# The last level of ranks as two half levels, in steps over two quads of buckets

## Chip, cores and metric

The kernel runs on one core of a Trainium2 chip. The metric is the device time of one execution in microseconds (us). Before the change it was 2584.67 us, the median of three runs between 2577.09 and 2587.84.

## What is computed

One layer of a graph network on 12,500 nodes of 64 features and 212,500 edges, the edges sorted by `dst`:

```python
def _L0_gnn_ref(h, row, col, dist, eW1, eb1, eW2, eb2, nW1, nb1, nW2, nb2):
    edge_in = jnp.concatenate([h[row], h[col], dist], axis=1)
    e = jax.nn.silu(edge_in @ eW1 + eb1)
    e = jax.nn.silu(e @ eW2 + eb2)
    agg = jax.ops.segment_sum(e, row, num_segments=h.shape[0])
    node_in = jnp.concatenate([h, agg], axis=1)
    return jax.nn.silu(node_in @ nW1 + nb1) @ nW2 + nb2
h = jnp.maximum(_layernorm(x, axis=-1), 0.0)
return x + _L0_gnn_ref(h, src, dst, edge_weight1, ...)
```

The sum goes over `row`, which is `src`, while the edges come sorted by `dst`. So each edge has to be brought to its source node.

## The kernel before, in words

**Blocks.** The edges are taken in 208 blocks of 1024. For a block, `count` (L337) counts on DVE and PE how many edges go to each of NB = 100 buckets of 125 nodes, and gives each edge a rank in its bucket; the running counts lie in SBUF in `base`. `send` (L406) multiplies on PE (`qp`, L418) the `dst` part of the first layer and the edge weight, copies the result on ACT to `qs` (L429, L435) and scatters it row by row to the table `q` in HBM with indirect DMAs on POOL (L442), eight of 128 rows for a full block. `send_all` (L463) cuts this work into pieces, three to a block.

**Levels.** In `q` each bucket has rows for 2304 ranks. `LEVELS` (L54) cuts the ranks into levels: each entry gives the number n of 128-rank tiles, the block after which the level's rows are complete, and a number of spare ranks. Spare ranks that a bucket does not fill are zeros, written in mid-run by `fill` (L106) from the ACT queue; when a level closes, `count` lifts `base` to the level's end (L377). The last level before is `(1, 208, 128)`: 128 ranks, complete after the last block.

**Batches and steps.** A quad is G = 4 buckets; there are 25. A batch is one level of one quad; `fetch` (L484) loads its rows as `qt` and the quad's `src` part of the first layer as `a`, on the SP queue, and in the last level also x and the normalised features for the node update (`nodes_in`, L226). A batch has n steps, each over four tiles of 128 edges: 450 steps in all. The parts of a step are:

- `s_lr` and `s_one_t`: the edges' node numbers, turned to lie along the free axis, compared on DVE with the partition number, which gives `oneT` (125 nodes x 128 edges a tile);
- `s_pt`: on PE `qt` transposed (L532) plus `a` times `oneT` (L538), which adds the source's part of the first layer; then Silu on ACT;
- `s_bias`, `s_p2`: the second layer (L570) and Silu;
- `s_one`: DVE compares node numbers (`one`, L551), and asks for the batch four ahead;
- `s_seg`: on PE the sums over the edges of a tile, `e2` times `one`, into the PSUM tile `seg` (L584; the pool `sg` has two buffers);
- `s_add`: DVE adds `seg` to the sums `aggT` in SBUF (L595); in the last level it also appends the quad's node update `nodes` (L235) to `tails`.

`nodes` is a generator in four parts: z (L242, L245) with Silu on ACT, o (L251), the addition of x on DVE (L254), and the output DMA.

**Order.** The order on PE, DVE, ACT and SP is written by the program itself. In one turn of the loop (L880) the parts of neighbouring steps stand in the order of `turn`; `None` is a hook, four to a turn:

```python
turn = [
    (s_pt, 1), (s_add, -2), (s_one_t, 2), None, (s_bias, 1), (s_p2, 0), (s_one, 0), None, (s_seg, -1), None, (s_lr, 3), None,
]
```

The number says how many steps ahead or behind a part is. At a hook the loop puts in pieces of later blocks, spread so that a goal is met when a level's first load is asked for, and one part of the first of `tails`. The goal for a level that needs the blocks up to `LEVELS[w][1]` is

```python
LEAD = 3 * PIECES
total = PIECES * (nblocks - 2 * FIRST)
goal_of = lambda w: min(PIECES * (LEVELS[w][1] - 2 * FIRST) + LEAD, total)
```

with PIECES = 3, FIRST = 4 and nblocks = 208. A load of rows waits for the last scatter of the block that its level names.

## Time and profile before

| what | value |
|---|---|
| runs | 2577.09, 2584.67, 2587.84 us |
| profiled execution: time | 2577.09 us |
| its span, first to last instruction | 2575.3 us |
| mean granted PE clock | 0.933 |
| busy: PE, PEld (weight loads) | 2162.4, 1981.9 us |
| busy: DVE, ACT, POOL | 2050.7, 1110.8, 1802.1 us |
| chain of waits by engine | PE 33%, DMA 20%, POOL 17%, DVE 14%, issue 9% |
| DMA | 457 MB, 177 GB/s over the span |

PE is the matmuls, PEld the loads of their stationary operands; an f32 matmul shows as two records of each. The span is cut into 40 slices of 64 us; each digit there is the busy share in tenths. In a timeline a row gives the start, the length, engine, line, operation, `out<-in`, the shape and the number of instructions merged, and in brackets how long the engine stood idle before and what released it. Matmuls overlap, so what one costs in a stream is read from the starts and not from the lengths.

### The profile page before, as it was taken

What the parts mean: (1) busy time and instruction counts of PE and PEld (TensorE: products, weight loads), DVE (VectorE), ACT (ScalarE), POOL (GpSimd) and SP (SyncE); (2) the same over time, 40 slices, a digit from 0 to 9 for tenths busy, and PEclk for the clock granted to TensorE, in tenths of its full rate; (3) what the DMA queues carried; (4) which work ended last, traced back from release to release, by engine and by line L of the source; (5) the groups of instructions that cost most, each with busy time, mean ns of one, the idle gap of its engine ahead of it and who ended that gap; (6) DMA issues with size and microseconds to landing.
All of it is one profiled execution on the core that took longest, in us unless ns stands there. A gap on an engine that the chain in (4) does not pass through costs nothing.

```text
span 2575.3 us, 45805 instructions
## 1 busy us (share of the span) xinstructions
PE 2162.4 (84%) x16192; PEld 1981.9 (77%) x16192; DVE 2050.7 (80%) x3413; ACT 1110.8 (43%) x2408; POOL 1802.1 (70%) x1712
## 2 busy tenths in 40 slices
PE   2575676656698898989999889999999999999997
PEld 1453676555588888888888888888899898899986
DVE  5986787766788888888898888888889899886542
ACT  2342343222244444444544444444455554444442
POOL 3777777777777777777777777777777777762110
PEclk9776898778899999999999999999999999999999
DMA  4463565555566665666544444454555556665642
GB/s 103 165 211 130 182 194 186 178 168 174 184 216 215 220 199 172 217 219 216 196 167 165 162 156 164 159 172 165 165 177 177 168 170 195 203 191 175 190 157 73
DMA packets 229455, 456.97 MB, mean 177 GB/s; under 512 B 43543, under 2 KB 87588, under 8 KB 229013
## 3 DMA queue, kind: packets, MB, share of 16 engines
q1 hardware_dynamic: 151033, 282.94, 34.1%
q0 software_dynamic: 53536, 123.03, 13.9%
q10 hardware_dynamic: 24650, 48.00, 6.2%
q8 instruction: 131, 2.15, 0.3%
q14 instruction: 105, 0.86, 0.1%
HBM read 264.26 MB, written 189.54 MB: 176 GB/s over the span
## 4 chain that ended last, share of the span: by engine, by line
PE 33%; DMA 20%; POOL 17%; DVE 14%; issue 9%; ACT 2%; DVEq 0%; SPq 0%; POOLq 0%; ACTq 0%
POOL q L442 17%; DMA q<-qs,to 16%; PE pt L538 7%; PE p L570 7%; PE seg L584 6%; PE qp L418 5%; PE pt L532 3%; DVE oneT L523 2%; DMA qt<-q 2%; PE lr L518 2%; DVE oh L345 2%; DVE each L353 2%; DMA pick<-in_edge_weight_dram 2%; DVE one L551 1%; DVE aggT L595 1%
## 5 line engine op out<-in xcount | busy, mean ns | idle before, releaser
L442 POOL DMA_INDIRECT q<-qs,to x1661 | 1773.0, 1067 | 607.7 <-issue 410.0
L542 ACT ACTIVATE e<-pt 128x512 f32<-128x512 f32 x450 | 268.7, 597 | 933.3 <-PE pt L538 933.3
L538 PE MATMUL pt<-oneT,a 125*128 125x128 f32 (+1 forms) x2400 | 493.4, 341 | 45.5 <-DVE oneT L523 45.4
L570 PE MATMUL p<-w,e 128*128 128x128 f32 x3600 | 502.1, 285 | 0.0
L570 PEld LDWEIGHTS p<-w,e 128*128 128x128 f32 x3600 | 480.8, 200 | 22.2 <-issue 7.4
L584 PE MATMUL seg<-one,e 128*128 128x125 f32 x3600 | 490.8, 281 | 3.0 <-DVE one L551 2.7
L418 PE MATMUL qp<-win,pick 128*128 128x256 f32 x1664 | 432.7, 407 | 61.7 <-DMA pick<-in_edge_weight_dram 40.4
L584 PEld LDWEIGHTS seg<-one,e 128*128 128x128 f32 x3600 | 451.1, 197 | 4.1 <-ACT p L564 1.5
L538 PEld LDWEIGHTS pt<-oneT,a 125*128 125x128 f32 x2400 | 367.3, 200 | 71.9 <-DVE oneT L523 54.3
L418 PEld LDWEIGHTS qp<-win,pick 128*128 128x128 f32 x1664 | 327.0, 206 | 110.5 <-issue 32.3
L429 ACT COPY qs<-qp 128x512 f32<-128x512 f32 x418 | 242.7, 583 | 348.4 <-PE qp L418 280.4
L523 DVE TENSOR_SCALAR oneT<-lr,part 125x512 f32<-125x512 f32 x450 | 335.0, 744 | 32.6 <-PE lr L518 32.3
L353 DVE TENSOR_REDUCE each<-oh 128x100 bf16<-128x800 bf16 x208 | 316.0, 1519 | 7.2
L551 DVE TENSOR_TENSOR one<-nodes,qt 128x500 f32<-128x500 f32 x450 | 302.8, 673 | 0.0
L532 PE MATMUL pt<-ident,qt 128*128 128x128 f32 x1800 | 283.7, 282 | 20.1 <-DVE oneT L523 19.5
L574 ACT ACTIVATE e<-p 128x512 f32<-128x512 f32 x450 | 268.2, 596 | 39.3 <-PE p L570 38.7
L564 ACT COPY p<-b2f 128x512 f32<-128x512 f32 x450 | 266.7, 593 | 0.0
L595 DVE TENSOR_TENSOR aggT<-aggT,seg 128x500 f32<-128x500 f32 x275 | 184.1, 669 | 74.9 <-PE seg L584 74.6
L400 DVE SCALAR_TENSOR_TENSOR to<-rank,offE 128x8 int32<-128x8 f32 x208 | 36.3, 175 | 246.9 <-DMA q<-qs,to 242.7
L518 PE MATMUL lr<-identb,qt 128*125 128x128 bf16 x1800 | 181.6, 225 | 41.9 <-DMA qt<-q 36.3
L532 PEld LDWEIGHTS pt<-ident,qt 128*128 128x128 f32 x1800 | 197.6, 146 | 22.5 <-DVE oneT L523 21.9
L398 DVE TENSOR_REDUCE rank<-mine 128x8 f32<-128x800 f32 x208 | 205.1, 986 | 7.2
(134 smaller groups left out, 1589.8 us busy)
## 6 DMA issues: line engine op xcount, KB each, us to landing
qt<-q SPq DMA_DIRECT2D x150, 576.0 KB
a<-ta SPq DMA_DIRECT2D x300, 256.0 KB
qt<-q SPq DMA_DIRECT2D x150, 288.0 KB
q<-zeros ACTq DMA_DIRECT2D x25, 1080.0 KB
q<-qs,to POOLq DMA_INDIRECT x1661
bc<-dests SPq DMA_DIRECT2D x103, 256.0 KB
q<-zeros ACTq DMA_DIRECT2D x10, 1440.0 KB
win<-tb SPq DMA_DIRECT2D x208, 58.0 KB
```

The costliest lines, as they stand in the source:

```text
L353: nc.vector.tensor_reduce(each, oh.rearrange("p t b -> p b t"), AX.X, OP.add)
L418: nc.tensor.matmul(qps[t // 2][:, t % 2, :k], pick[:, t * P : (t + 1) * P], win[:, :k], start=True, stop=True)
L442: ins = nc.gpsimd.indirect_dma_start(out=q[:], out_offset=bass.IndirectOffsetOnAxis(ap=to[:k, j : j + 1], axis=0), in_=qs[:k, t % 2, a, :] ...
L523: nc.vector.tensor_scalar(oneT, st[k].pop("lr")[:L], part1[:L, :], None, op0=OP.is_equal)
L532: nc.tensor.matmul(pt[:, t, :], qt[:, j, :H], ident, is_transpose=True, start=t == 0, stop=False, skip_group_check=True)
L538: nc.tensor.matmul(pt[:, cols, :], a[:L, b, :], oneT[:, cols, :], start=False, stop=True, skip_group_check=True)
L542: nc.scalar.activation(e1, pt, AF.Silu)
L551: nc.vector.tensor_tensor(one.rearrange("p (b j) l -> p b j l", j=n), nodes1[:, None, None, :].to_broadcast(wide), loc[:, tiles[0][1] : ti ...
L564: nc.scalar.copy(p2, b2f)
L570: nc.tensor.matmul(p2[:, t, :], e1[:, t, :], w2, start=False, stop=t == G - 1, skip_group_check=True)
L574: nc.scalar.activation(e2, p2, AF.Silu)
L584: nc.tensor.matmul(item[2][:, b, :], e2[:, t, :], one[:, t, :], start=j < G, stop=j >= G * (n - 1))
```

## The change

The last entry of `LEVELS` becomes two of half a tile, 64 ranks each, complete after blocks 205 and 208, both with 64 spare ranks. For these two levels a batch takes two quads (the 25th quad stands alone), so that there are 13 batches of one step in each and 451 steps in all. A tile of 128 edges now holds 64 ranks of one bucket in its first half and 64 of another in its second half. So:

- `fetch` loads each quad's rows in two DMAs of 64 partitions, and `a` for eight buckets in one DMA, in its own pool of three buffers; `fetch_to` asks for batches NH = 3 ahead where they have two quads, and loads what the node update needs one batch ahead, in the second half level only;
- in `s_pt` each tile has two matmuls of 64 columns with `a` of two buckets;
- in `s_seg` each tile has two matmuls of 64 rows, one for each half, into two PSUM tiles; `s_add` adds both;
- a hook takes up to two parts from the first of `tails`.

The running counts in SBUF, the two buffers of `sg` and the loads of the edge weights ahead of the counts, which the change's short description names as well, are the same in both kernels.

```diff
-LEVELS += [(1, 184, 0), (1, 194, 32), (1, 202, 96), (1, 208, 128)]
-ENDS = [P * sum(n for n, _, _ in LEVELS[: w + 1]) for w in range(len(LEVELS))]
+LEVELS += [(1, 184, 0), (1, 194, 32), (1, 202, 96), (0.5, 205, 64), (0.5, 208, 64)]
+ENDS = [int(P * sum(n for n, _, _ in LEVELS[: w + 1])) for w in range(len(LEVELS))]
...
-        batches = [(w, B, n) for w, (n, _, _) in enumerate(LEVELS) for B in range(NB // G)]
-        steps = [(w, B, n, g) for w, B, n in batches for g in range(n)]
+        batches = []
+        for w, (n, _, _) in enumerate(LEVELS):
+            m = 2 if n < 1 else 1
+            batches += [(w, B, n, min(m, NB // G - B)) for B in range(0, NB // G, m)]
+        number = {(w, B): i for i, (w, B, _, _) in enumerate(batches)}
+        steps = [(w, B, n, g) for w, B, n, _ in batches for g in range(max(1, n))]
...
+            rows = G * int(n * P)
+            for b in range(B, B + m):
+                at = b * G * ROWS + G * ENDS[c] - rows
+                if n < 1:
+                    for h in range(2):
+                        part_ = q[at : at + rows, :].rearrange("(r h j) w -> r h (j w)", h=2, j=2)[:, h, :]
+                        to = qt[h * HB : (h + 1) * HB, 2 * (b - B) : 2 * (b - B) + 2, :]
+                        load_ready(c, nc.sync.dma_start(to.rearrange("p j w -> p (j w)"), part_).ins)
...
+            a = (ld2 if m == 1 else ld3[0]).tile([P, m * G, H], F32, name=f"a{m}")
+            nc.sync.dma_start(a, ta_buckets[:, B * G : (B + m) * G])
...
+        def fetch_to(i):
+
+            while fetched[0] < len(batches) and fetched[0] <= i + (NQ if batches[fetched[0]][3] == 1 else NH):
+                fetch(fetched[0])
+                fetched[0] += 1
+            while fetched[1] < min(fetched[0], i + NH - 1):
+                _, B, _, m = batches[fetched[1]]
+                for b in range(B, B + m):
+                    node_in[b] = nodes_in(b, ndp[0])
+                fetched[1] += 1
...
+            for t, h in itertools.product(range(nt), range(2)) if steps[k][2] < 1 else ():
+                cols = slice(h * HB, (h + 1) * HB)
+                b = t // 2 * G + 2 * h + t % 2
+                nc.tensor.matmul(
+                    pt[:, t, cols], a[:L, b, :], oneT[:, t, cols], start=False, stop=True, skip_group_check=True
+                )
...
+                item[2] = [sgp.tile([P, G, L], F32, name="seg") for _ in range(2 if n < 1 else 1)]
             e2, one = st[k].pop("e2"), st[k].pop("one")
+            for t, h in itertools.product(range(len(tiles)), range(2)) if n < 1 else ():
+                rows = slice(h * HB, (h + 1) * HB)
+                nc.tensor.matmul(
+                    item[2][h][:, t, :], e2[rows, t, :], one[rows, t, :], start=True, stop=True
+                )
...
+            for h, seg in enumerate(segs):
+                v = aggT[:, B * G : (B + m) * G, :]
+                if n < 1:
+                    v = v.rearrange("p (q h j) l -> p h q j l", h=2, j=2)[:, h]
+                    seg = seg[:, : 2 * m, :].rearrange("p (q j) l -> p q j l", j=2)
...
-                    if tails and next(tails[0], 0) == 0:
-                        tails.pop(0)
+                    for _ in range(min(2, len(tails))):
+                        if tails and next(tails[0], 0) == 0:
+                            tails.pop(0)
```

## Prediction

> **What bounds the kernel now.** I read first the page's row of slices, to see which engine is full when.

> ```profile
> PE   2575676656698898989999889999999999999997
> POOL 3777777777777777777777777777777777762110
> PEclk9776898778899999999999999999999999999999
> ```

> POOL shows a steady 7 until about slice 36 (some 2300 us) and then nothing: a 7 that never moves is an engine that never pauses for long. POOL's own timeline says so, at the place where this ends:

> ```profile
> 2250.84 0.96 POOL L442 DMA_INDIRECT q<-qs,to  x1 [0.30 <-DMA q<-qs,to]
> ...
> 2328.59 0.97 POOL L442 DMA_INDIRECT q<-qs,to  x1 [14.78 <-ACT qs L435]
> ```

> Up to 2297 us POOL issues scatter after scatter with 0.30 us between. From record to record, in hundreds from the first at 49 us on, the mean interval is 1.34 to 1.40 us, with one slower hundred at the start. So until 2297 us POOL sets the pace. After that it waits 4 to 15 us at a time for ACT, which waits for PE; its last scatter starts at 2397 us. Who is full then is in the windows (length, then PE, PEld, DVE, ACT, POOL busy, granted clock, DMA share, GB/s):

> ```profile
> 2200.00:2297.00 97.00, 88.57 (x767) 85.38 (x766) 85.37 (x140) 45.44 (x94) 73.37 (x71) 0.98 0.62 197
> 2297.00:2400.00 103.00, 102.05 (x951) 100.93 (x950) 70.39 (x117) 50.54 (x104) 30.34 (x30) 1.00 0.56 177
> 2414.00:2545.00 131.00, 131.00 (x1074) 116.06 (x1072) 52.84 (x90) 54.65 (x112) 15.97 (x22) 1.00 0.49 154
> ```

> From 2297 us on PE is busy all the time at full clock, and nothing else is near full: the last two levels are paced by PE alone, its instructions in order. So each instruction added to PE there lengthens the run, and nothing is gained by readier data. The price of a turn of the step loop is read from PE's timeline, as the start of one row less the start of the next. First a turn of the last level but one, then one of the last level, which carries a quad's node update (z, z, o) too:

> ```profile
> 2405.31 0.39 PE L518 MATMUL lr<-identb,qt 128*125 128x128 bf16 x4
> 2405.54 0.61 PE L532 MATMUL pt<-ident,qt 128*128 128x128 f32 x4
> 2405.98 1.06 PE L538 MATMUL pt<-oneT,a 125*128 125x128 f32 x8
> 2406.88 1.06 PE L570 MATMUL p<-w,e 128*128 128x128 f32 x8
> 2407.77 1.06 PE L584 MATMUL seg<-one,e 128*128 128x125 f32 x8
> 2408.66 0.39 PE L518 MATMUL lr<-identb,qt 128*125 128x128 bf16 x4
> ...
> 2490.94 1.01 PE L242 MATMUL z<-aggT,w1g 128*128 128x250 f32 x4
> 2491.88 0.69 PE L245 MATMUL z<-hrn,w1n 64*128 64x250 f32 x4
> 2492.50 1.16 PE L570 MATMUL p<-w,e 128*128 128x128 f32 x8
> 2493.50 0.98 PE L251 MATMUL o<-w2n,zs 128*125 128x64 f32 x8
> 2494.32 1.11 PE L584 MATMUL seg<-one,e 128*128 128x125 f32 x8
> 2495.26 0.39 PE L518 MATMUL lr<-identb,qt 128*125 128x128 bf16 x4
> ```

> A plain turn is 2408.66 - 2405.31 = 3.35 us. A turn with nodes is 5.89 us (its lr starts at 2489.37). Each f32 matmul shows as two records, so pt's four are x8: 0.90 us, 0.11 us a record. The last level is 25 such turns, 25 x 5.89 = 147 us.

> **The change part by part.**

> *The split itself.* The last level's 128 ranks become 64 due at block 205 and 64 due at block 208. The earlier due time should let work start before the last blocks. It does not: goal_of is min(3 x (due - 8) + 9, 600), with LEAD 9. Due 205 gives 600 and due 208 is cut to 600, so before the first load of the split levels all pieces are sent in either kernel. The built order agrees: PE's, SP's and POOL's operations are the same, one for one, up to the first step of the split levels; DVE has one extra closing test, four small operations, near block 205 (and three in mid-run, all under 0.4 us each). What waited here before was one load on SP, 2.3 us, of which PE saw 1.0 us; at most that is won, and I count 0. ACT gets five more zero fills of half size, done in mid-run like the others; issue takes 0.31 us each, and POOL's interval is 1.34 to 1.39 us in the hundreds with fills and 1.36 to 1.40 after them, so 0.

> *pt (64-column matmuls).* A full step now has 8 matmuls of 64 columns for 4 of 128: 16 records for 8. Each loads its own 125x128 weights. The nearest row is o: 125 weight columns, 64 moving columns, 8 records in 2494.32 - 2493.50 = 0.82 us, 0.1025 each, scarcely less than 0.1125 at 128 columns. The weight load sets this rate, not the stream. So 16 records take 1.64 us (o's rate) to 1.80 us (pt's own); I take 1.72, +0.82 a full step. There are 12 full and one half step in each half level, 25 full ones in all: +20.5 us. Lower bound: nothing, if half the columns take half the time, as gaps of 55 ns that occur once in each o group would have it; upper bound +22.5.

> [...]

> *seg (half rows).* 8 matmuls of 64 rows for 4 of 128, halves in turn, into two PSUM tiles. One after the other they would take 16 x 0.1125, +0.9 us. But the early products of 64 rows show what two halves do:

> ```profile
> 181.43 1.26 PE L200 MATMUL ab<-w,hr 64*128 64x128 f32 x16 [0.81 <-ACT hr L634]
> 182.65 0.44 PE L630 MATMUL ht<-ident,xs 128*128 128x128 f32 x2
> ```

> Sixteen records in 1.22 us, though only two following each other on the same rows are 0.11 us apart: the halves run beside each other. So seg keeps 8 slots, plus the way in and out of half rows. That price is in the z rows: 250-column records go at 0.213 us; around L245 the gaps are 0.303 in and 0.299 out (+0.09 each), its first inner gap 0.31 for 0.21 (+0.10) and p's first gap after it 0.214 for 0.112 (lr is bf16, so +0.08 there, an estimate): 0.36 us a step. In the first half level that is 13 x 0.36 = 4.7 us. In the second, one node update's L245 stands directly before seg, so one way in and out serves both: 0. Bounds: 0, and 25 x 0.9 + 4.7 = 27 us if the halves do not overlap.

> *DVE.* aggT is added to twice a step, 52 adds for 25, 27 x 0.675 = 18 us more, hidden under PE: a turn needs 2 x 0.675 + 0.744 + 0.67 = 2.8 us of 4.5. seg's two tiles now take both buffers, so seg waits for the adds of the step before; these end about 1.6 us into the turn, seg starts about 3.1 us into it. If that cover were gone, each late us costs 26.

> *SP and DMA.* Loads are four of 72 KB and one of 512 KB for each two quads: 126 issues for 50, at 0.32 to 0.43 us. 5 issues are 1.7 us of a 4.5 us turn; in the second half with x, hd and out, 15 issues are 5.6 us of 9.3. Table rows are loaded twice, +6.4 MB: 807 KB a turn is 178 GB/s, where the page has slices of 215 to 220. A load still waits for the DVE comparison four steps back, about 1.3 turns before its use. Price 0; if late by 0.5 us a turn, +13.

> *Nodes.* Twice as many per hook: in the steady order z and o stay apart, by pt or seg. At the start of the second half z and o adjoin twice (0.6 us each by the row below), at the end four times; before, the end had these waits, 3.5 us:

> ```profile
> PE z L242 <- DVE aggT L595: 2.3, 3, 0.8
> PE o L251 <- ACT zs L247: 1.2, 2, 0.6
> ```

> 6 x 0.6 = 3.6 for 3.5: 0.

> **Sum.** First half: 12.5 x (3.35 + 0.82) + 4.7 = 56.8; second: 12.5 x (3.35 + 0.82 + 2 x 2.54) = 115.6, 2.54 being 5.89 - 3.35. 172 for 147: +25 us. The profiled execution took 2577.1 us (span 2575.3 and 1.8 around it), which would become 2602. It was the fastest of three; the median is 2584.7, so 2610.

> **The rivals.**
> *Half price for half columns*: pt costs nothing, +5, 2590. For it the single 55 ns gaps; against it the other gaps in o, near 0.11 us. 0.12.
> *Halves in series, or late buffers*: seg +22 more, or seg and pt waiting for adds and loads up to 0.9 us a turn: 2632 to 2645. Against it the 181 us row; but there both halves came with all inputs ready. 0.18.
> *Faster: POOL's pace*. Place: 49 to 2297 us. Other lanes for DMA waits after the fills and other tile addresses could shorten the scatter interval; 0.01 us is 16 us over 1600 scatters. It decides from 1.345 us mean (now about 1.37), which cancels +25; 1.337 gives 2572. For it, hundreds at 1.34; against it, the same order on every engine there. 0.08.

> **How the numbers follow.** Forecast 0.62, with its own range 2600 to 2622 (the runs of before spread over 11 us). The range of 8 in 10 takes in part of the half-price case and part of the serial one: 2593 to 2636. About 0.5%, 13 us, is what a measurement of this kernel tells from no change: faster 0.07 (POOL), same 0.13 (half price, and a little of POOL), slower 0.80.

> **What would show it.** The last scatter still near 2397 us. Then PE at 100%, turns of 4.5 us in the first half and 9.3 in the second; pt of 16 records in 1.64 to 1.80 us; seg of 16 records in about 0.9 to 1.3; PE waits for DMA or aggT under 5 us after 2400. Wrong would be: pt near 0.9 us, seg near 1.8, PE idle between turns, or a scatter interval below 1.35.

## The result, and the profile after

Before 2586.26 us (median of 4 runs), after 2624.14 us (4 runs, 2618.65 to 2624.32): the ratio is 1.0147 [1.0117, 1.0177], so the change costs about 38 us, where +25 was forecast. 2624.14 us lies within the stated range, 2593 to 2636, and 2 us above the forecast's own, 2600 to 2622. The profiled execution of after took 2624.24 us, its span 2622.5.

The page's slices of after, in the order in which they were shown of before:

```profile
PE   2574776665698898989899989999999999999997
POOL 3777777777777777777777777777777777732010
PEclk9677888778899998999999999999999999999989
```

POOL keeps its 7 up to the same slice, and PE is near full from there on, as before. New in the part that the change touches is the 8 of the clock in the last slice but one, 2491 to 2557 us, where before had a 9. In POOL's timeline the last scatter is this:

```profile
2405.89 1.29 POOL L442 DMA_INDIRECT q<-qs,to  x1 [0.30 <-issue]
```

It starts at 2405.9 us, 9 later than in before. Runs of kernels whose order is before's up to here put it anywhere from 2396.9 to 2410.4 us (before 2396.9, and two experiments below, 2397.8 and 2410.4), and four of the experiments on after put it at 2401.4 to 2407.1 us, so these 9 us lie within the spread of single runs and show no shift by the change. What the change does is therefore counted from the first `pt` of the last level to the end of the span: 166.4 us in before, 203.7 in after, +37.3.

PE's timeline of after: one turn of the first half level, and the start of the second.

```profile
2431.52 0.44 PE L543 MATMUL lr<-identb,qt 128*125 128x128 bf16 x4
2431.80 0.61 PE L558 MATMUL pt<-ident,qt 128*128 128x128 f32 x4
2432.24 1.90 PE L565 MATMUL pt<-oneT,a 125*128 125x64 f32 x16
2433.98 1.11 PE L614 MATMUL p<-w,e 128*128 128x128 f32 x8
2435.02 1.16 PE L629 MATMUL seg<-one,e 64*128 64x125 f32 x16
2436.11 0.44 PE L543 MATMUL lr<-identb,qt 128*125 128x128 bf16 x4
...
2485.34 0.30 PE L543 MATMUL lr<-identb,qt 128*125 128x128 bf16 x2 [0.60 <-DMA qt<-q]
2491.00 0.30 PE L543 MATMUL lr<-identb,qt 128*125 128x128 bf16 x2 [1.15 <-DMA qt<-q]
2492.03 0.30 PE L543 MATMUL lr<-identb,qt 128*125 128x128 bf16 x2 [0.73 <-DMA qt<-q]
2492.16 0.61 PE L558 MATMUL pt<-ident,qt 128*128 128x128 f32 x4
2492.60 3.22 PE L565 MATMUL pt<-oneT,a 125*128 125x64 f32 x16
2495.62 1.98 PE L242 MATMUL z<-aggT,w1g 128*128 128x250 f32 x4
...
2525.97 0.39 PE L543 MATMUL lr<-identb,qt 128*125 128x128 bf16 x4
...
2535.24 0.39 PE L543 MATMUL lr<-identb,qt 128*125 128x128 bf16 x4
```

From start to start, the turn is 2436.11 - 2431.52 = 4.59 us (3.35 in the last level but one). `pt`'s 16 records take 2433.98 - 2432.24 = 1.74 us where 8 took 0.90. `seg`'s 16 records take 1.09 us: the halves run beside each other. The rest of the turn's increase, 4.59 - 3.35 - 0.84 = 0.40 us, is the way in and out of half rows, but for some 0.05 us that experiment 1 has with `pt` alone. So far each term of the sum is close to its forecast.

What was not forecast are the waits in the rows behind. PE waits three times for `qt`, 2.48 us in all, and after the third wait `pt` takes 3.0 us from start to start for the same 16 records. The windows of after say why (length, then PE, PEld, DVE, ACT, POOL busy, granted clock, DMA share, GB/s):

```profile
2418.73:2476.42 57.69, 57.69 (x600) 55.06 (x598) 30.74 (x50) 20.73 (x39) 0.00 (x0) 1.00 0.62 179
2476.42:2492.60 16.18, 13.70 (x139) 12.73 (x138) 8.15 (x15) 4.60 (x9) 2.95 (x4) 1.00 0.71 210
2492.60:2507.41 14.81, 14.26 (x66) 11.37 (x65) 2.78 (x5) 2.51 (x5) 2.89 (x4) 0.54 0.51 154
2507.41:2583.10 75.69, 74.95 (x640) 64.50 (x639) 25.80 (x48) 26.66 (x56) 11.60 (x16) 1.00 0.52 152
```

In the first half level PE never stops. At the start of the second it stands idle for 16.18 - 13.70 = 2.48 us, and in the next 14.81 us its granted clock is 0.54; at most 14.81 x 0.46 = 6.8 us of that is lost. Then it is at full clock again, with turns of 2535.24 - 2525.97 = 9.27 us (9.25 forecast). Why `qt` is late there is in the timeline of SP's queue, where the length is how long an issue takes (first a load of before's):

```profile
2400.80 0.32 SPq L493 DMA_DIRECT2D qt<-q  x1
...
2443.33 2.36 SPq L503 DMA_DIRECT2D qt<-q  x4
2445.79 0.54 SPq L508 DMA_DIRECT2D a<-ta  x1
2447.91 2.37 SPq L503 DMA_DIRECT2D qt<-q  x4
...
2478.38 0.87 SPq L118 DMA_DIRECT2D xr<-in_x_dram  x2
2479.30 0.34 SPq L232 DMA_DIRECT2D hrn<-hd  x1
2479.69 0.87 SPq L118 DMA_DIRECT2D xr<-in_x_dram  x2
2480.60 0.34 SPq L232 DMA_DIRECT2D hrn<-hd  x1
2481.06 2.47 SPq L503 DMA_DIRECT2D qt<-q  x4
...
2487.18 2.98 SPq L503 DMA_DIRECT2D qt<-q  x4
```

A load of 64 partitions takes about 0.59 us to issue (2.36 for four), where before's load of 128 partitions took 0.32. Its source rows also have a stride now; which of the two makes the issue longer was not tried. Four of them and `a` make 2.9 us a turn, which fits into 4.59. At the start of the second half level two quads' x and normalised features come to it in each turn, four loads for x and two for the features, 2.4 us: 5.3 us a turn, while the turns around the change of level, from 2472.66 to 2484.41 us, have no node updates yet and take PE 3.5 to 4.1 us. Later turns take 9.27 us, and SP has time again.

### The profile page after: what moved, and what is told of

It is laid out like the page before. It is cut to its first block, busy times and chain, and to the rows that moved or that the text cites. A ratio compares the mean times of both kernels' runs of the same rounds, so it can differ in the third digit from the quotient of the medians.

```text
span 2622.5 us, 46834 instructions
## 1 busy us (share of the span) xinstructions
PE 2195.8 (84%) x16592; PEld 2009.5 (77%) x16592; DVE 2067.2 (79%) x3449; ACT 1113.9 (42%) x2411; POOL 1809.3 (69%) x1712
## 3 DMA queue, kind: packets, MB, share of 16 engines
q0 software_dynamic: 53536, 123.03, 13.7%
## 4 chain that ended last, share of the span: by engine, by line
PE 34%; DMA 20%; POOL 17%; DVE 13%; issue 8%; ACT 2%; DVEq 0%; SPq 0%; POOLq 0%; ACTq 0%
DMA q<-qs,to 17%; POOL q L442 17%; PE p L614 6%; PE pt L571 6%; PE seg L635 5%; PE qp L418 4%; PE pt L558 3%; DVE oneT L549 2%; DMA qt<-q 2%; DVE each L353 2%; DVE oh L345 2%; PE lr L543 2%; PE pt L565 2%; DVE one L595 1%; DVE aggT L651 1%
## 5 line engine op out<-in xcount | busy, mean ns | idle before, releaser
L442 POOL DMA_INDIRECT q<-qs,to x1661 | 1780.2, 1072 | 609.2 <-issue 415.5
L571 PE MATMUL pt<-oneT,a 125*128 125x256 f32 (+1 forms) x2200 | 467.2, 346 | 49.2 <-DVE oneT L549 49.1
L635 PE MATMUL seg<-one,e 128*128 128x125 f32 x3400 | 462.8, 280 | 5.3 <-DVE one L595 2.5
L635 PEld LDWEIGHTS seg<-one,e 128*128 128x128 f32 x3400 | 426.5, 197 | 6.4 <-ACT e L618 2.9
L571 PEld LDWEIGHTS pt<-oneT,a 125*128 125x128 f32 x2200 | 342.4, 200 | 75.3 <-DVE oneT L549 57.7
L595 DVE TENSOR_TENSOR one<-nodes,qt 128x500 f32<-128x500 f32 x425 | 286.0, 673 | 0.0
L651 DVE TENSOR_TENSOR aggT<-aggT,seg 128x500 f32<-128x500 f32 (+1 forms) x302 | 198.8, 666 | 93.3 <-PE seg L635 60.6
```

The source lines that it names most:

```text
L442: ins = nc.gpsimd.indirect_dma_start(out=q[:], out_offset=bass.IndirectOffsetOnAxis(ap=to[:k, j : j + 1], axis=0), in_=qs[:k, t % 2, a, :] ...
L571: nc.tensor.matmul(pt[:, cols, :], a[:L, b, :], oneT[:, cols, :], start=False, stop=True, skip_group_check=True)
L595: nc.vector.tensor_tensor(one.rearrange("p (b j) l -> p b j l", j=n), nodes1[:, None, None, :].to_broadcast(wide), loc[:, tiles[0][1] : ti ...
L635: nc.tensor.matmul(item[2][0][:, b, :], e2[:, t, :], one[:, t, :], start=j < G, stop=j >= G * (n - 1))
```

## The experiments

Eight more kernels were run, each against before on the same chip: the first four with its median at 2581.80 us (13 runs), the others at 2584.01 (8 runs). "Tail" is the time from the start of the last scatter to the end of the span, 178.4 us in before and 216.6 in after; tails, turns and waits are read from one trace of each kernel.

**1. `pt` alone, in before.** The last level keeps its 25 steps, but each `pt` matmul is cut into two of 64 columns with the same weights.

```diff
+            last = steps[k][0] == len(LEVELS) - 1
+            for t, h in itertools.product(range(G), range(2)) if last else ():
+                cols = slice(h * HB, (h + 1) * HB)
+                nc.tensor.matmul(
+                    pt[:, t, cols], a[:L, tiles[t][1], :], oneT[:, t, cols], start=False, stop=True, skip_group_check=True
+                )
-            for b, same in itertools.groupby(range(G), lambda t: tiles[t][1]):
+            for b, same in itertools.groupby(range(G), lambda t: tiles[t][1]) if not last else ():
```

> The kernel before, with pt of its last level in two matmuls of 64 columns a tile on the same table rows (nothing is left out). Measure: from the start of the last scatter to the end of the span, 178.4 us before, 216.6 after the change. Theory, the weight load sets the price of a 64-column matmul: pt takes 1.72 us for 0.90 in 25 turns, +20 us, tail 199 us, ratio 1.008. Rival, half the columns at half the price: pt stays near 0.9 us, tail 178 to 181, ratio 1.00.

Measured: 2608.69 us (2600.3 to 2610.09), ratio 1.0101 [1.0071, 1.0132]; tail 200.7 us. Its PE timeline:

```profile
2490.76 1.90 PE L538 MATMUL pt<-oneT,a 125*128 125x64 f32 x16
2492.49 1.07 PE L242 MATMUL z<-aggT,w1g 128*128 128x250 f32 x4
```

1.73 us for `pt` from start to start, 0.83 more than with 8 records, and turns of 6.78 us for 5.89. From the first `pt` of the last level to the 25th, 24 turns, it is 154.9 us for 133.5: +21.4 us, 0.89 a turn, and the tail, with the 25th, is 22.3 us longer. Half the columns are not half the price.

**2. `seg` alone, in before.** Each `seg` matmul becomes two of 64 rows into two PSUM tiles, which `s_add` adds one after the other.

```diff
...
+            for t, h in itertools.product(range(G), range(2)) if c == len(LEVELS) - 1 else ():
+                rows = slice(h * HB, (h + 1) * HB)
+                nc.tensor.matmul(
+                    item[2][h][:, tiles[t][1], :], e2[rows, t, :], one[rows, t, :], start=True, stop=True
+                )
...
```

> The kernel before, with seg of its last level in two matmuls of 64 rows a tile into two PSUM tiles, both added on DVE (nothing is left out). Theory, halves run beside each other and only the way in and out costs, 0.40 us a turn as the first half level after the change shows: +10 us, tail 188 us, ratio 1.004. Rival, halves in series: seg near 1.8 us, +23 us, tail 201. Rival, the second add or the lack of a free PSUM tile holds up PE: PE waits for aggT in every turn, some 0.7 us, +17 us on top.

Measured: 2597.82 us (10 runs, 2590.85 to 2607.14), ratio 1.0061 [1.0046, 1.0076]; tail 195.0 us. In its PE timeline, a steady turn and the end:

```profile
2494.10 1.16 PE L585 MATMUL seg<-one,e 64*128 64x125 f32 x16
2495.19 0.44 PE L518 MATMUL lr<-identb,qt 128*125 128x128 bf16 x4
...
2578.38 1.79 PE L242 MATMUL z<-aggT,w1g 128*128 128x250 f32 x4 [1.54 <-DVE aggT L602]
```

16 records in 1.09 us, and turns of 6.27 to 6.28 us, +0.39 each: the steady cost is the one forecast for half rows, and in the steady turns no `z` waits for an add. From the first `pt` of the last level to the 25th that is +8.4 us. The rest of the tail's +16.6, 7 us more than was expected, is at the end, where three `z` wait 4.6 us in all (2.3 in before) until the second add is done, and the clock then falls:

```profile
2578.00:2594.00 16.00, 12.34 (x49) 8.53 (x49) 2.52 (x5) 1.66 (x4) 0.00 (x0) 0.52 0.03 9
```

So halves in series, at +22 us, are ruled out; the rival of the second add came true only at the end.

**3. Relief for SP, by ACT.** In after, the loads for the node update go to ACT's queue.

```diff
-        rows16(nc.sync.dma_start, xr, x_rows[:, b : b + G, :])
+        rows16(nc.scalar.dma_start, xr, x_rows[:, b : b + G, :])
...
-        nc.sync.dma_start(hr, hd[:, b // 2 : b // 2 + G // 2, :])
+        nc.scalar.dma_start(hr, hd[:, b // 2 : b // 2 + G // 2, :])
```

> The changed kernel, with the loads for the node updates issued from the ACT queue and not from SP. Theory, at the start of the second half level SP has more to issue (5.4 us a turn) than a turn lasts (4.6 us, 3.4 with a half step), the rows of the next batch come late, PE waits 2.5 us, and its clock falls to half for 13.7 us, which costs 7 us more: with SP relieved, no half clock near that place, PE waits there under 0.5 us, tail 207 us for 216.6. Rival, the loads are late by the transfers themselves or by the wait for the last scatter: same waits, same half clock, tail 215 to 218.

Measured: 2632.20 us (2625.25 to 2634.26), ratio 1.0184 [1.015, 1.0219]; tail 229.0 us, 12 longer than after's. The waits of PE from 2476 us on:

```profile
PE o L251 <- ACT zs L247: 17.9, 15, 3.1
PE lr L543 <- DMA qt<-q: 0.8, 1, 0.8
```

The waits for `qt` are nearly gone, as they should be, but the issues now stand in ACT's own order, ahead of the Silu that `o` waits for: 17.9 us. The edit moved the late work to another engine, and says nothing of the size of the loss.

**4. Fewer issues.** In after, one load for both halves of a tile instead of two.

```diff
-                    for h in range(2):
-                        part_ = q[at : at + rows, :].rearrange("(r h j) w -> r h (j w)", h=2, j=2)[:, h, :]
-                        to = qt[h * HB : (h + 1) * HB, 2 * (b - B) : 2 * (b - B) + 2, :]
-                        load_ready(c, nc.sync.dma_start(to.rearrange("p j w -> p (j w)"), part_).ins)
+                    part_ = q[at : at + rows, :].rearrange("(r h j) w -> h r (j w)", h=2, j=2)
+                    to = qt[:, 2 * (b - B) : 2 * (b - B) + 2, :].rearrange("p j w -> p (j w)")
+                    load_ready(c, nc.sync.dma_start(to, part_).ins)
```

> The changed kernel, with each quad's rows loaded by one DMA over 128 partitions and not two over 64. Theory as in the run before it: SP issues 1.2 us less a turn (4.2 us for 5.4 us), PE waits under 1 us at the start of the second half level, no half clock there, tail 207 us; the turns of the first half level stay at 4.58 us. Rival, SP's issue is not the cause: tail 215 to 218.

Measured: 2696.75 us (2692.68 to 2701.84), ratio 1.0435 [1.0403, 1.0468]; tail 292.9 us. Neither theory had this. The DMA view from 2440 to 2452 us, in 40 slices of 0.3 us, and the waits of PE from 2420 us on:

```profile
DMA  1111111111111118957997211111111111111111
GB/s 50 50 46 50 50 50 48 55 55 55 49 42 50 46 50 145 155 159 296 428 393 239 66 50 50 46 50 50 50 46 50 52 58 55 55 45 38 50 50 46
```

```profile
PE lr L542 <- DMA qt<-q: 38.2, 22, 3.0
```

Except for a burst, when `a` is loaded, little over a tenth of the 16 DMA engines is busy and 50 GB/s flow: from 2440 to 2444.4 us, 30 packets of 1152 bytes (`qt`) a microsecond at 51 ns each, and 4 of 4096 bytes at 163 ns, together two engines' worth. The source's slowest dimension is here `h`, of size 2, as many as the engines that are kept busy; that the one sets the other was not tried by itself. The experiment measured this pattern and not SP's issues, which it left open.

**5. The node loads earlier.** In after, the first eight quads' x and features are loaded one a turn during the first half level, where SP has time, and the others when after loads them.

```diff
...
-            while fetched[1] < min(fetched[0], i + NH - 1):
-                _, B, _, m = batches[fetched[1]]
-                for b in range(B, B + m):
-                    node_in[b] = nodes_in(b, ndp[0])
-                fetched[1] += 1
+            first_, end_ = number[len(LEVELS) - 2, 0], number[len(LEVELS) - 1, 0]
+            goal = min(8, i - first_ - 1) if i < end_ + 3 else min(NB // G, 2 * (i - end_ + 2))
+            while len(nodes_of) < goal:
+                nodes_of.append(len(nodes_of))
+                node_in[nodes_of[-1]] = nodes_in(nodes_of[-1], ndp[0])
```

> The changed kernel, with the node loads of the first eight quads issued one quad a turn in the first half level, so that SP has none to issue at the start of the second. Theory, as for the two runs before that were meant to relieve SP: a turn of the first half level has 4.6 us and SP 2.95 + 1.2 us to issue, the rows come in time, PE waits under 0.5 us at the start of the second half level, no half clock there; tail (last scatter to the end) 207 us for 216.6. Rival, the rows are late for another reason: tail 214 to 218 with the half clock as it was.

Measured: 2619.28 us (2617.13 to 2620.04), ratio 1.0134 [1.0107, 1.016]; tail 208.5 us. The window at the start of the second half level, and all of PE's waits from 2470 to 2520 us:

```profile
2478.00:2494.00 16.00, 16.00 (x160) 15.07 (x159) 9.20 (x16) 5.20 (x10) 0.00 (x0) 1.00 0.76 219
```

```profile
PE o L251 <- ACT zs L247: 1.3, 3, 0.6
```

PE is busy without a gap, no wait for `qt` is left there, and the stretch of low clock is gone. From the first `pt` of the last level to the end it takes 195.3 us, 8.4 less than after and 28.9 more than before. So that start costs 8.4 us in these traces, and the remaining +28.9 is close to the forecast sum. The medians moved by less (38 us above before's in after, 35 here), and the intervals of the two ratios overlap: the size rests on one trace of each.

**6. Without the half matmuls.** Experiment 5, with `pt` in four matmuls of 128 columns, all with the `a` of the first bucket, and `seg` in four of 128 rows, whose one sum is added for both. So it leaves out the second bucket's `a` and the separate sums.

```diff
-            for t, h in itertools.product(range(nt), range(2)) if steps[k][2] < 1 else ():
-                cols = slice(h * HB, (h + 1) * HB)
-                b = t // 2 * G + 2 * h + t % 2
+            for t in range(nt) if steps[k][2] < 1 else ():
+                b = t // 2 * G + t % 2
...
-                    pt[:, t, cols], a[:L, b, :], oneT[:, t, cols], start=False, stop=True, skip_group_check=True
+                    pt[:, t, :], a[:L, b, :], oneT[:, t, :], start=False, stop=True, skip_group_check=True
...
-            for t, h in itertools.product(range(len(tiles)), range(2)) if n < 1 else ():
-                rows = slice(h * HB, (h + 1) * HB)
-                nc.tensor.matmul(
-                    item[2][h][:, t, :], e2[rows, t, :], one[rows, t, :], start=True, stop=True
-                )
+            for t in range(len(tiles)) if n < 1 else ():
+                nc.tensor.matmul(item[2][0][:, t, :], e2[:, t, :], one[:, t, :], start=True, stop=True)
```

> As the run with early node loads, and pt in four matmuls of 128 columns (the second 64 edges of a tile get the table rows of the first bucket), seg in four of 128 rows into one PSUM tile (both halves summed together, the same sums added to both buckets): parts of the computation are changed. Theory, pt, seg and the late start are the whole of the loss: tail 178 to 182 us, as before the change (178.4). Rival, the doubled table loads, the doubled adds or the order of the node updates cost something of their own: tail 185 or more.

Measured: 2601.20 us (5 runs, 2597.09 to 2607.39), ratio 1.0071 [1.0047, 1.0095]; tail 192.1 us, 16.4 below experiment 5 and so 10 to 14 above what was expected: the rival, 185 or more, came true. PE's waits from 2400 us on, and SP's queue in one turn:

```profile
PE lr L543 <- DMA qt<-q: 9.3, 14, 1.7
```

```profile
2442.62 2.37 SPq L503 DMA_DIRECT2D qt<-q  x4
2445.09 0.52 SPq L508 DMA_DIRECT2D a<-ta  x1
2445.66 1.66 SPq L118 DMA_DIRECT2D xr<-in_x_dram  x2
2447.36 0.34 SPq L232 DMA_DIRECT2D hrn<-hd  x1
2447.80 2.38 SPq L503 DMA_DIRECT2D qt<-q  x4
```

A turn of PE is down to 3.35 us again, and now SP's issues set the pace where a quad's node loads are among them, 5.2 us from `qt` to `qt` in the rows shown and 4.4 in most others: 9.3 us of waits. So the half matmuls' price in PE's time was also the cover of the half loads' price in SP's. Without the half matmuls and without the waits, some 4 us remain over before (192.1 - 9.3 - 178.4 = 4.4). `pt` and `seg` together are then worth 16.4 + 9.3 = 25.7 us, near the 22.3 and 13 x 0.39 = 5.1 of experiments 1 and 2.

**7. The split made to start early.** Experiment 5, with a goal of one block's pieces instead of `LEAD` ahead of the first half level, so that it can begin before the last block is sent.

```diff
-        goal_of = lambda w: min(PIECES * (LEVELS[w][1] - 2 * FIRST) + LEAD, total)
+        goal_of = lambda w: min(PIECES * (LEVELS[w][1] - 2 * FIRST) + (PIECES if w == 11 else LEAD), total)
```

> As the run with early node loads, and the goal at the start of the first half level is block 205 and one block more, not all 208, so that the last two blocks are sent during the first half level: what the earlier due time was made for. Theory, PE paces everything from 2297 us on, so moving pieces past the start of the level gains nothing: same time as the run with early node loads, within 4 us; PE stays full. Rival, work starts sooner on rows that are ready and the whole becomes shorter by the 10 us or more for which POOL now waits on PE.

Measured: 2618.58 us (2611.03 to 2626.17), ratio 1.0129 [1.0092, 1.0166], against 1.0134 of experiment 5. Its last scatter starts at 2464.6 us, some 58 us later than in experiment 5 (2406.8) and in the middle of the first half level, and it ends at the same time (span 2617.8 us, 2615.3 there). PE did not stay full: at the start of the level it waits 2.4 us for `qt`, and its clock is 0.50 for the 6.8 us from 2417.0 on, which costs at most 3.4 us. So the rival's gain of 10 us or more is not there, as PE has the same work either way; one of up to some 6 us could be hidden behind these losses.

**8. A part of the node update made early.** In before, the features' part of the node update is multiplied early, where the features are made: instead of `hd`, a table `yd` with that product is kept, and in the last level DVE adds it to `z`. This takes the four `z` records of L245, with half rows, out of every turn of the last level, and `o` comes one hook later, behind `seg`.

```diff
...
-            nc.tensor.matmul(z[a], w1g, aggT[:, b + a : b + G : 2, :], start=True, stop=False)
+            nc.tensor.matmul(z[a], w1g, aggT[:, b + a : b + G : 2, :], start=True, stop=True)
...
-            nc.tensor.matmul(z[a], w1n[half, :], hr[half, :, :L], start=False, stop=True)
+            nc.vector.tensor_tensor(zs[:, a], z[a], y[:, a], op=OP.add)
...
-            nc.sync.dma_start(hd[:, b // 2 : (b + G) // 2, :], hr)
+            yr = fp.tile([P, 2, G // 2, L], F32, name="yr")
+            for a in range(2):
+                half = slice(a * D, (a + 1) * D)
+                yp = mm.tile([P, G // 2, L], F32, name="yp", tag="mm")
+                nc.tensor.matmul(yp, w1n[half, :], hr[half, :, :L], start=True, stop=True)
+                nc.scalar.copy(yr[:, a], yp)
+            nc.sync.dma_start(yd[:, b // G, :], yr.rearrange("p a i l -> p (a i l)"))
...
```

> The kernel before, with the part of the node update that does not need the sums (w1n times the features) computed early, when the features are made, kept in HBM, and added on DVE in the last level; nothing is left out. Theory, in the last level only PE counts: a turn loses L245 and its way in and out, 0.62 + 0.09 + 0.10 us, so 5.9 us becomes 5.1, tail 178.4 to 159 us, ratio 0.992. Rival, the early work falls on a stage that sets the pace, or DVE and ACT between z and o hold up PE: turn over 5.5 us or the scatters end over 10 us later, ratio 0.998 or more.

Measured: 2561.23 us (2557.9 to 2567.01), ratio 0.9915 [0.9887, 0.9944]; tail 158.9 us, 19.5 less than before. A turn in its PE timeline:

```profile
2489.75 0.39 PE L517 MATMUL lr<-identb,qt 128*125 128x128 bf16 x4
...
2490.43 1.06 PE L537 MATMUL pt<-oneT,a 125*128 125x128 f32 x8
2491.32 1.01 PE L242 MATMUL z<-aggT,w1g 128*128 128x250 f32 x4
2492.17 1.05 PE L569 MATMUL p<-w,e 128*128 128x128 f32 x8
2493.06 1.05 PE L583 MATMUL seg<-one,e 128*128 128x125 f32 x8
2493.95 0.99 PE L251 MATMUL o<-w2n,zs 128*125 128x64 f32 x8
2494.77 0.39 PE L517 MATMUL lr<-identb,qt 128*125 128x128 bf16 x4
```

5.02 us from `lr` to `lr`, for 5.89. The version is faster than before and after. The product made early costs nothing that can be seen: the last scatter starts at 2397.2 us, before's at 2396.9. It is the reading of the prediction's first part, used the other way round: where PE alone sets the pace, an instruction less on PE is time won.

## Why the prediction was right, and where it was short

- *What bounds the last stage.* Right. PE is busy for all 57.69 us of the first half level's window, and in experiment 7 the split starts early without a gain that shows, as the prediction's "0" for the split itself had it.
- *`pt`.* Right in size: 1.74 us for 16 records where 1.72 was taken, and +22.3 us measured by itself in experiment 1, for +20.5. The rival of half price for half columns falls with it, and so does its sum of +5 us: no run shows `pt` at no extra price. With a weight load for each matmul, 64 columns take 0.108 us a record and 128 take 0.112, and PEld is busy for all of both stretches, 1.74 us in after and 0.90 in before. That the weight load sets this rate was not tried by itself; no fixed price of a record does, since `seg`'s 16 records of half rows go at 1.09 / 16 = 0.068 us.
- *`seg`.* Right in steady state: the halves run beside each other, and a step pays 0.39 us (experiment 2) to 0.40 (after), for 0.36. The rival of halves in series falls.
- *The second half's turn.* 9.27 us, for 9.25: as one way into half rows for both `z` and `seg` had it.
- *SP and DMA.* This is the step that was short. It read "Price 0; if late by 0.5 us a turn, +13", and rested on issues of 0.32 to 0.43 us, five of them 1.7 us of a turn. The loads of half the partitions take about 0.59 us each, so that a turn has 2.9 us of issues. That still fits into a steady turn, as forecast, but not into the turns at the change of level, which carry the node loads and have no node updates yet. There the late loads cost 2.48 us of waits and up to 6.8 at low clock; loading the first quads' node inputs earlier took 8.4 us away (experiment 5), and experiment 6 shows the same queue as the bound when PE's turns are short. The bound of 13 us was of the right order, but it was put down as an unlikely loss in every turn and not looked for at one place.
- *The other 3.9 us.* After experiment 5's edit, +28.9 us are left for +25 forecast: 1.8 in `pt` (0.89 us a turn for 0.82), at most 0.5 in `seg` (13 steps of 0.04); the rest, some 1.6 us, was not taken apart.
- *POOL's pace.* The scatter's spread from run to run, 2396.9 to 2410.4 us for the same order, is half of what this rival needed to cancel the loss; nothing shows a shift by the change. Its sum was off: at the 16 us for 0.01 us that it states, 1.345 us for 1.37 is 40 us, and 1.355 would have cancelled +25.
- *The signs named.* They were too weak for this: PE's waits for `qt` after 2400 us add up to 3.2 us, within the 5 that were allowed, while the low clock that followed them was not among the signs.
- *Luck.* There is some: the number is inside the range because that was widened to 2636 us for halves in series, which did not come; without the late loads at the change of level, some 8 us, it would have been inside the forecast's own.

The least foreseen part is the low clock. In after it follows three waits of 0.60, 1.15 and 0.73 us within 7.3 us. But in experiment 6 waits of 0.79, 1.66 and 0.76 us within 7.2 us leave the clock at 1.00. By their length alone the waits in after would be a loss of 2.48 us; experiment 5 took 8.4 us away with them, about 6 more.

The traces say more when they are divided as the clock divides them. In all ten, from 300 us on, it changes between 1.00 and 0.50 only at the ends of equal steps of 3.41 us. Of the steps at full clock there, all 347 in which PE was busy for under 42% were followed by one at half clock, 48 of the 122 with 42 to 50%, and 6 of the 5663 with more (in before and after alone all 74, 7 of 18 and none of 1126). In some 150 of the 347 no wait was as long as 3.41 us, and in 12 none as long as 2: in these, several shorter waits stand in one step. The two waits before the fall in after do so too, and in experiment 6 they are split between steps:

```profile
2489.51:2492.92 3.41, 1.53 (x19) 1.00 0.67 168
2444.86:2448.27 3.41, 1.69 (x15) 1.00 0.81 219
```

The first row is of after, PE alone: busy for 1.53 us, 45%, and the clock falls at its end. The second is the emptiest step of experiment 6 at those waits, just under 50%, and it does not. Both are in the range that goes either way, so this pair alone proves nothing. How long the clock stays low is open: of 323 steps at half clock with PE busy throughout, 306 were followed by full clock (59 of 61 in before and after), and the 17 others, two of them in after, all lie behind 2400 us in kernels with half matmuls. That the waits cause the low clock was not tried by itself; experiment 5 took both away together.

## What to carry to other kernels

Where one engine alone sets the pace of a stage, count its instructions and its weight loads, and don't take half the columns or rows for half the price (here 0.108 us a record with 64 columns for 0.112 with 128, and 0.39 us more a step with half rows); a stage that is made ready earlier, in more and smaller pieces, pays for the pieces, and the gain lies in work that can be moved to a stage where that engine has room (19.5 us of the tail in experiment 8). When a load is cut in two, count the issue time of its queue turn by turn (here 0.59 us for each half and 0.32 for the whole), at the change from one stage to the next above all, where the loads of the new stage come before its longer turns do. And don't price a short wait of PE by its length alone (here 13.7 us at a clock of 0.50 came after 2.48 us of waits): look at what other waits lie within a few microseconds of it, and at the granted clock of the 15 us behind.
